# Norms applied behind the products, scan terms added in pairs and later state copies in a hybrid convolution, scan, attention and expert kernel

## The chip, the cores and the metric

The kernel runs on one core of a Trainium2 chip. The core has TensorE (PE, with its weight loads shown apart as PEld), VectorE (DVE), ScalarE (ACT), GpSimd (POOL) and SyncE (SP), which issues the transfers. All data is 32-bit floating point. The metric is the device time of one execution in microseconds (us); lower is better.

## The reference

The input is four images of 128 channels, 64 by 64 pixels. Two layers follow. In the first, per image:

```python
xn  = _ln(xp, ln_w, ln_b)                    # after a group norm of x
h   = depthwise 3x3 convolution, _ln, gelu, 1x1 convolution; y = y + h
m   = _mamba(chunks of _ln(y)) + skip_scale * chunks
out = _ln(inp + cat, ln_w, ln_b) @ proj_w.T + proj_b
x   = x + out
```

The scan inside `_mamba` runs over 4096 pixels with 16 states for each of 64 inner channels, in four chunks of the channels:

```python
h = dA_t * h + dBu_t
y = jnp.einsum('bdn,bn->bd', h, C_t)
```

In the second, on tokens `t` (pixels by 128 channels):

```python
t = t + attention(_ln_t(t))                  # 4 heads, 4096 keys, softmax
n = _ln_t(t)
p = top 2 of softmax(n @ router_w + router_b), shares that sum to 1
t = t + sum over the two experts of p * (n @ expert_w[e] + expert_b[e])
```

`_ln` takes off the mean over the channels and multiplies by rstd = 1/sqrt(variance + eps). In the norm ahead of `proj_w`, weight and bias follow it; the norm ahead of the router and the experts has none.

## The kernel before

An image is cut into 8 blocks of 512 pixels (`BLK`), a block into `NT` = 4 tiles of 128. Four images make 32 blocks.

The main loop of the kernel counts *slots*. In each slot every engine gets its instructions in program order; `Queue` and `queued` (lines 428 to 448) keep that order on each engine. All instructions issued this way bear the profile's line L445, so groups are told apart by the names of tiles.

**The scan** is cut into 512 *units* `(b, i, p, n)`: image, block, half of the channels and pair of states. A unit takes two slots. In its even slot `driven` (DVE) makes `h` as a product of fetched rows and `du`, and `scan` (DVE) runs over 1025 columns: two states laid end to end. In its odd slot `read` (DVE) multiplies `h` by other rows into `hc`, 128 by 2 by 512. The decays `da` are two ScalarE exponentials, issued a slot or two ahead by `prepared`; `carried` copies the second state's start into `h`, and `kept` copies both end states out, at the end of the unit's even slot. The terms `hc` of 8 units sum in one PSUM tile `y`: `turned_on` (line 792) transposes four tiles of each half of `hc` with accumulation. Half 0 is due one slot after `read`, half 1 two slots after. When a group of 8 units is done, ScalarE copies `y` to `yT`, and a slot later `turned_back` transposes it and calls `summed_up`, whose first step `scanned` (DVE) reads the result.

**Attention** runs beside it, one group per slot, 1024 in all: four score products `sc` (PE), two exponentials `pT` of 128 by 1024 (ACT), and in the next slot the value products `av` (PE, eight half products). There are two score buffers. Attention for an image begins when its first blocks are `closed`, so it trails the scan; from `END`, 1024 slots, attention runs alone.

**Two lanes, X and Y,** carry all other work as generators; each half of `advance` runs a lane to its next `yield`. Per block, Y runs `first_norm`, `conv` and `inputs`, which makes the scan's inputs, with a chain of five POOL operations ending in `du`. X runs `closed` (line 816), which makes the output projection, the residual and keys, queries and values, and `finished` (line 1059), which applies the attention's output projection, the router and the experts. A lane has one PSUM tile, `work(lane)`. In `closed` and `inputs` the set `held` keeps the two lanes from using X's tile at once.

`normalised` (line 504) is the norm in both lanes: `bn_stats` and `bn_aggr` (DVE) on four tiles, `rs` and `shift` (DVE), the power -1/2 and a product on POOL, then, two yields on, four ScalarE activations into `xt`. Its caller transposes `xt`. `closed` uses it twice, `finished` once. In `closed` the first result is transposed, scaled by `lnw` and `lnb` into `f` (ACT), multiplied by `projT`, and added to `xr`, which holds x and `projb`. In `finished` the transposed result `xf` goes to the router `rw` and, times each expert's share, to `ew`. The shares go through DRAM (`shares`) to be spread over the partitions. The output `res` begins as a ScalarE copy of a PSUM tile, in which the biases `eb8` times the shares and the transposed `acc`, as products with the identity, are summed.

One order in an even slot, as issued: `da` (ACT), `driven` (DVE), X's second half, scores (PE), exponentials (ACT), `scan` (DVE), Y's first half, `turned_back`, `turned_on` (PE), Y's second half, `kept` (ACT), values (PE), X's first half.

Of the kernel before, what the change touches and what calls it, by code (L numbers as in the profile page):

```python
# [36 lines left out]
def conv_mamba_attn_moe_kernel(ctx: ExitStack, tc: tile.TileContext, t: dict):  # L37
# [65 lines left out]
    with (  # L103
        tc.tile_pool(name="bound", bufs=1) as bd,
        tc.tile_pool(name="ps_w", bufs=2, space=PSUM) as ps_w,
    ):
        pw = ps_w.tile([P, P], F32, name="pw")
        nc.tensor.matmul(pw, lhsT=xdt, rhs=dtT, start=True, stop=True)
        nc.vector.tensor_copy(wdt, pw)
        pw = ps_w.tile([P, P], F32, name="pw")  # L110
        nc.tensor.matmul(pw[0:1, :], lhsT=bvc, rhs=wp, start=True, stop=True)
        crow1 = bd.tile([1, C], F32, name="crow1")
        nc.vector.tensor_add(crow1, pw[0:1, :], bp)
        pw = ps_w.tile([P, P], F32, name="pw")
        nc.tensor.matmul(pw, lhsT=ones, rhs=crow1, start=True, stop=True)
        nc.vector.tensor_copy(crow, pw)

        sq = bd.tile([P, 2 * NH + 1], F32, name="sq")
        nc.vector.memset(sq, 0.0)
        bsq = bd.tile([DH, 2 * NH], F32, name="bsq")
        for i, (w, bias) in enumerate(((wqn, bqn), (wkn, bkn))):
            for h in range(NH):
                r = slice(DH * h, DH * h + DH)
                pw = ps_w.tile([P, P], F32, name="pw")
                nc.tensor.matmul(pw[0:DH, 0:DH], lhsT=w[:, r], rhs=w[:, r], start=True, stop=True)
                g = bd.tile([DH, DH], F32, name="g", bufs=2)
# [40 lines left out]
        nc.vector.tensor_copy(general, ok)  # L170
    setup.close()


# [327 lines left out]
    def by_tile(src):  # L501
        return src.rearrange("p (j c) -> p j c", c=P)

    def normalised(lane, src):


        st = small.tile([P, NT, 6], F32, name=f"st{lane}")
        mv = small.tile([P, NT, 2], F32, name=f"mv{lane}")
# [3 lines left out]
            vector.bn_aggr(out=mv[:, j, :], in_=st[:, j, :])  # L512
        rs = small.tile([P, NT], F32, name=f"rs{lane}")
        vector.tensor_scalar_add(rs, mv[:, :, 1], EPS)
        shift = small.tile([P, NT], F32, name=f"shift{lane}")
        vector.tensor_scalar_mul(shift, mv[:, :, 0], -1.0)
        gpsimd.tensor_tensor(rs, rs, mhalf, ALU.pow)
# [283 lines left out]
    def summed_up(b, i, p, y):  # L801
        scanned(b, i, p, y)
        done.add(("scan", b, i, p))
        if p == 1:
            lanes["X"].appendleft((("closed", b, i), closed(b, i), []))

    def turned_back(b, i, p, yT):
        y = ps_y.tile([P, BLK], F32, name="y")
        for j in range(NT):
            tensor.transpose(y[:, j * P : (j + 1) * P], yT[:, j * P : (j + 1) * P], ident)  # L810
        summed_up(b, i, p, y)

    vst = side.tile([P, NH, NT, 2 * DH], F32, name="vst")
    gpsimd.memset(vst[:, :, :, DH:], 1.0)
# [1 line left out]
    def closed(b, i):  # L816
# [25 lines left out]
        vector.tensor_add(cm, ps, cm)  # L842
        gpsimd.tensor_add(by_tile(xr), by_tile(xr), projb[:, None, :].to_broadcast([P, NT, C]))
        yield
        while held:
            yield
            yield
        held.add("closed")
        ps = transposed("X", by_tile(cm))
        yield  # L850
        xt = yield from normalised("X", by_tile(ps))
        held.clear()
        ps = transposed("X", xt)
        yield
        f = tmp("X", "f")
        scalar.activation(f, ps, AF.Identity, bias=lnb, scale=lnw)
        yield
        ps = work("X", [P, NT, C])
        for j in range(NT):
            mm(ps[:, j, :], f[:, j * P : (j + 1) * P], projT)  # L860
        yield
        tt = side.tile([P, NT, C], F32, name="tt")
        vector.tensor_add(tt, ps, by_tile(xr))
        send(tsave[b][:, s], tt.rearrange("p j c -> p (j c)"), 2)
        xt = yield from normalised("X", tt)

# [192 lines left out]
    def finished(b, qb, lane):  # L1059
# [18 lines left out]
            mm(ps[:, j, :], aT[:, j * P : (j + 1) * P], wp)  # L1078
        yield
        vector.tensor_add(acc, ps, acc)  # L1080
        xt = yield from normalised(lane, acc)
        ps = transposed(lane, xt)
        yield
        xf = tmp(lane, "xf")
        scalar.copy(xf, ps)
# [8 lines left out]

        yield

        pr = routed("pr")
        vector.tensor_add(pr, ps, rb[:, None, :].to_broadcast(wide))
# [28 lines left out]
        vector.tensor_mul(pr, pr, top1.to_broadcast(wide))  # L1127
        yield

        ps = work(lane)  # L1130
        for j in range(NT):
            tensor.transpose(ps[0:NE, j * P : (j + 1) * P], pr[:, j, :], ident)
        yield
        prT = tmp(lane, "prT")[0:NE, :]
        scalar.copy(prT, ps[0:NE, :])
        shares = dram.tile([NE, BLK], F32, name=f"shares{lane}")
        send(shares, prT)
        yield

        def share(e):  # L1140
# [10 lines left out]


        ps = work(lane)
        mm(ps, eb8, prT, True, False)
        for j in range(NT):
            mm(ps[:, j * P : (j + 1) * P], acc[:, j, :], ident, False, j == NT - 1)
        yield
        res = tmp(lane, "res")
        scalar.copy(res, ps)
        yield  # L1160
        ahead = deque(share(e) for e in (0, 2))
        yield
# [23 lines left out]
    def advance(lane, second):  # L1186
# [3 lines left out]
        while True:  # L1190
            if lane not in running:

                tasks = lanes[lane] if lanes[lane] or slot < END else lanes["X"]
                if not tasks or not all(k in done for k in tasks[0][2]):
                    return False

# [89 lines left out]
    def ends(unit):  # L1286
        return unit[3] == NST - 2

    waiting = None

    while slot < END or due or closing or waiting or left or later or lanes["X"] or running:
        at, odd = divmod(slot, 2)
        flush()
        if slot == 0:
# [6 lines left out]
        if unit and not odd:  # L1301
            h = h_of.pop(at)
            driven(unit, h, rows.pop((at, 0)))
        advance("X", True)
        group = next(groups, None)
        if group:
# [144 lines left out]
```

## Time and profile before

| | us |
|---|---|
| median of 3 runs | 5390.83 |
| lowest and highest of them | 5374.57, 5391.15 |
| the profiled execution's own time | 5380.67 |
| its span, first to last instruction | 5378.9 |
| first scan starts at | 101.1 |
| first score product at | 382.9 |
| last scan ends at | 4790.1 |

The mean granted TensorE clock is 0.951. The page in slices of 134.5 us (busy tenths) shows how the span falls into a start, a long even middle and an end without scans:

```profile
PE   4556898999999999999999999999999999999997
PEld 2333444444444444444444444444444444444443
DVE  4888767777777778877778778777777877751332
ACT  3456777888777788788877788787777787766553
POOL 2333233333322224223322324333322232310100
```

A line of the page's groups reads: line, engine, operation, what it writes and reads, shapes, count, then busy us and mean ns of one, then the idle time of the engine just before these instructions and what ended it. A line of waits reads: who waited for whom, us in total, times, longest.

### The profile page before, as it was taken

To read this page: it belongs to the slowest core of one execution; us is meant where nothing else is said; L and a number is where in the kernel's file an instruction comes from. 1 tells how busy PE (TensorE), PEld (TensorE's weight loads), DVE (VectorE), ACT (ScalarE), POOL (GpSimd) and SP (SyncE) were. 2 spreads that over 40 slices of the span, in tenths; PEclk is the share of its full clock that TensorE was granted. 3 is DMA by queue.
4 is the path that set the end of the run, shared out by engine and by line. 5 is a ranking of instruction groups with operands and counts; after the bars stand their busy time and mean duration, and the time that the engine had idled before them with its cause. 6 is when DMAs were issued, how large, how long until landed. Compare 5 with 4: busy or idle time off the path is not lost. (4 is left out here: it accounts for less than half of the span.)

```text
span 5378.9 us, 64061 instructions
## 1 busy us (share of the span) xinstructions
PE 4850.0 (90%) x21066; PEld 2366.3 (44%) x21066; DVE 3757.2 (70%) x5123; ACT 3926.8 (73%) x6117; POOL 1525.0 (28%) x1091
## 2 busy tenths in 40 slices
PE   4556898999999999999999999999999999999997
PEld 2333444444444444444444444444444444444443
DVE  4888767777777778877778778777777877751332
ACT  3456777888777788788877788787777787766553
POOL 2333233333322224223322324333322232310100
PEclk7677899999999999999999999999999999999998
DMA  3556567667666667666766667666766676655532
GB/s 95 176 186 208 197 205 242 231 228 240 232 209 215 218 218 258 225 223 233 257 216 213 217 221 251 233 207 240 270 205 202 207 237 218 239 191 174 174 138 70
DMA packets 451702, 1131.71 MB, mean 210 GB/s; under 512 B 51985, under 2 KB 135330, under 8 KB 451362
## 3 DMA queue, kind: packets, MB, share of 16 engines
q1 hardware_dynamic: 450194, 1126.74, 62.4%
q8 instruction: 169, 2.77, 0.2%
q14 instruction: 171, 1.40, 0.1%
q10 hardware_dynamic: 1168, 0.80, 0.0%
HBM read 967.12 MB, written 143.39 MB: 206 GB/s over the span
## 5 line engine op out<-in xcount | busy, mean ns | idle before, releaser
L445 ACT ACTIVATE pT<-sc 128x1024 f32<-128x1024 f32 x2048 | 1985.7, 1024 | 637.2 <-PE sc L445 635.5
L445 PE MATMUL av<-pT,v 128*64 128x512 f32 x8192 | 2011.1, 612 | 16.7 <-ACT avs L445 16.4
L445 PE MATMUL sc<-qs,ks 128*128 128x512 f32 x4096 | 1316.7, 440 | 134.4 <-ACT pT L445 82.1
L445 DVE TENSOR_TENSOR_SCAN h<-da,state,h 128x1025 f32<-128x1025 f32 x512 | 1275.5, 2491 | 198.2 <-ACT h L445 168.9
L445 PEld LDWEIGHTS sc<-qs,ks 128*128 128x128 f32 x4096 | 705.6, 192 | 835.6 <-ACT pT L445 376.0
L445 PEld LDWEIGHTS av<-pT,v 128*64 128x64 f32 x8192 | 503.4, 138 | 824.7 <-issue 780.0
L445 ACT ACTIVATE da<-delta,amat 128x512 f32<-128x512 f32 x1024 | 747.9, 731 | 4.5 <-POOL delta L445 2.6
L445 DVE TENSOR_TENSOR h<-rows,du 128x1024 f32<-128x1024 f32 x512 | 707.8, 1382 | 53.0 <-POOL du L445 28.5
L445 DVE TENSOR_TENSOR hc<-rows,h 128x1024 f32<-128x1024 f32 x512 | 700.9, 1369 | 18.2 <-PE y L445 4.4
L445 PE MATMUL y<-ident,hc 128*128 128x128 f32 x4096 | 639.5, 285 | 64.3 <-DVE hc L445 56.9
L445 PEld LDWEIGHTS y<-ident,hc 128*128 128x128 f32 x4096 | 523.5, 147 | 269.2 <-issue 116.7
L445 POOL TENSOR_TENSOR rsX<-rsX,mhalf 128x4 f32<-128x4 f32 x92 | 232.7, 2530 | 843.1 <-DVE shiftX L445 843.1
L445 ACT ACT_TABLE_LOAD x319 | 409.3, 1283 | 18.1 <-PE ps_Y L445 13.5
L445 POOL TENSOR_TENSOR rsY<-rsY,mhalf 128x4 f32<-128x4 f32 x100 | 171.5, 1715 | 795.7 <-DVE shiftY L445 795.7
L445 ACT COPY state<-h 128x2 f32<-128x2 f32 x448 | 87.8, 196 | 416.3 <-DVE h L445 412.4
L445 POOL TENSOR_TENSOR avs<-avs,prev 128x512 f32<-128x512 f32 x96 | 153.0, 1594 | 660.2 <-ACT avs L445 612.6
L445 POOL TENSOR_TENSOR zs<-xin,zs 128x512 f32<-128x512 f32 x64 | 105.0, 1640 | 806.5 <-DVE xin L445 797.2
L445 POOL TENSOR_SCALAR du<-e 128x512 f32<-128x512 f32 x64 | 130.3, 2035 | 554.6 <-ACT e L445 554.6
L445 DVE TENSOR_TENSOR share<-share,xf 128x1024 f32<-128x1024 f32 x128 | 177.9, 1390 | 150.9 <-DMA share<-sharesX 124.9
L445 PE MATMUL ps_X<-share,w_ew 128*128 128x512 f32 x432 | 214.5, 619 | 1.7
L445 DVE TENSOR_TENSOR res<-res,ps_X 128x512 f32<-128x512 f32 x108 | 73.4, 679 | 178.9 <-PE ps_X L445 126.9
L445 ACT ACTIVATE xt<-ps_Y,shiftY,rsY 128x128 f32<-128x128 f32 x380 | 143.0, 466 | 67.9 <-POOL shiftY L445 60.7
(238 smaller groups left out, 4415.9 us busy)
## 6 DMA issues: line engine op xcount, KB each, us to landing
rows<-bcd SPq DMA_DIRECT2D x1024, 512.0 KB
ks<-kd SPq DMA_DIRECT2D x192, 512.0 KB
qs<-qd SPq DMA_DIRECT2D x161, 512.0 KB
share<-sharesX SPq DMA_DIRECT2D x108, 512.0 KB
v<-vd SPq DMA_DIRECT2D x192, 256.0 KB
ks<-kd SPq DMA_DIRECT2D x128, 256.0 KB
avd<-avs SPq DMA_DIRECT2D x96, 256.0 KB
prev<-avd SPq DMA_DIRECT2D x96, 256.0 KB
```

The costliest lines, as they stand in the source:

```text
L445: return lambda *args, **kw: queued(op(*args, **kw))
```

## The change

1. **Weights centred, rstd at eviction.** In the setup, a matrix `cen` (identity less 1/128) multiplies `rw`, `ew` and `projT` (the last scaled by `lnw`); `lnb` times `projT` is added to `projb`. A product of such a weight with data that still has its mean gives the product of the centred data. `moments` is split off `normalised`; `spread` computes rstd alone.
2. In `closed`, the first norm's `xt`, its transposition and `f` go; `projT` multiplies `cm`, and four DVE steps multiply by rstd and add `xr`. The wait for `held` goes.
3. In `finished`, `xt` goes; `acc` itself is transposed to `xf`. The router's result is multiplied by rstd (DVE). Shares are made twice, plain (for the biases) and times rstd (for the experts), in one tile `both`, and transposed together. The four products of `acc` with the identity go: `res` is the bias product plus `xf`, on DVE.
4. **Pairs.** From slot `ALONE` = 64 on, POOL adds the two halves of `hc` and one half is transposed, due two slots after `read`, three for the first unit of a group. Before slot 64, half 0 of a group's first unit becomes due two slots later.
5. `kept` runs at the end of the unit's odd slot. `summed_up` runs a slot after `turned_back`.
6. Lane Y does not take a `closed` task of X's once the scans are over.

```diff
+        def centred(w, src):
+            n = w.shape[1]
+            for k in range(0, n, P):
+                pw = ps_w.tile([P, P], F32, name="pw")
+                m = min(P, n - k)
+                nc.tensor.matmul(pw[:, 0:m], lhsT=cen, rhs=src[:, k : k + m], start=True, stop=True)
+                nc.vector.tensor_copy(w[:, k : k + m], pw[:, 0:m])
...
+    def spread(lane, src):
+
+        mv, rs = moments(lane, src)
+        gpsimd.tensor_tensor(rs, rs, mhalf, ALU.pow)
+        return rs
...
-        while held:
-            yield
-            yield
-        held.add("closed")
         ps = transposed("X", by_tile(cm))
         yield
-        xt = yield from normalised("X", by_tile(ps))
-        held.clear()
-        ps = transposed("X", xt)
-        yield
-        f = tmp("X", "f")
-        scalar.activation(f, ps, AF.Identity, bias=lnb, scale=lnw)
+        rs = spread("X", by_tile(ps))
         yield
         ps = work("X", [P, NT, C])
         for j in range(NT):
-            mm(ps[:, j, :], f[:, j * P : (j + 1) * P], projT)
+            mm(ps[:, j, :], cm[:, j * P : (j + 1) * P], projT)
         yield
         tt = side.tile([P, NT, C], F32, name="tt")
-        vector.tensor_add(tt, ps, by_tile(xr))
+        for j in range(NT):
+            vector.scalar_tensor_tensor(
+                tt[:, j, :], ps[:, j, :], rs[:, j : j + 1], xr[:, j * P : (j + 1) * P],
+                ALU.mult, ALU.add,
+            )
...
-        xt = yield from normalised(lane, acc)
-        ps = transposed(lane, xt)
+        rs = spread(lane, acc)
+        yield
+        ps = transposed(lane, acc)
...
-        mm(ps, eb8, prT, True, False)
-        for j in range(NT):
-            mm(ps[:, j * P : (j + 1) * P], acc[:, j, :], ident, False, j == NT - 1)
+        mm(ps, eb8, prT[0:NE, :])
         yield
         res = tmp(lane, "res")
-        scalar.copy(res, ps)
+        vector.tensor_add(res, ps, xf)
...
+        if summing:
+            summed_up(*summing)
+            summing = None
...
-            late = slot >= ALONE and unit[3] == 0
-            due.append((slot + 1 + late, unit, 0, hc[:, 0, :], False))
-            due.append((slot + 2, unit, 1, hc[:, 1, :], ends(unit)))
+            late = 2 * (unit[3] == 0)
+            if slot < ALONE:
+                due.append((slot + 1 + late, unit, 0, hc[:, 0, :], False))
+                due.append((slot + 2, unit, 1, hc[:, 1, :], ends(unit)))
+            else:
+                gpsimd.tensor_add(hc[:, 0, :], hc[:, 0, :], hc[:, 1, :])
+                due.append((slot + 2 + late // 2, unit, 0, hc[:, 0, :], ends(unit)))
         advance("Y", False)
         while closing and closing[0][0] <= slot:
-            turned_back(*closing.popleft()[1:])
+            summing = turned_back(*closing.popleft()[1:])
...
-        if unit and not odd:
+        if unit and odd:
             kept(unit, h)
```

More of the change, by code (lines that the diff above doesn't have):

```diff
@@ L170, in conv_mamba_attn_moe_kernel @@
         nc.vector.tensor_copy(general, ok)
+        cen = bd.tile([P, P], F32, name="cen")
+        nc.vector.tensor_scalar(cen, ident, 1.0 / C, None, ALU.subtract)
+        def centred(w, src):
[5 more added lines that the diff above has]
+                nc.vector.tensor_copy(w[:, k : k + m], pw[:, 0:m])
+        centred(rw, rw)
+        ewf = ew.rearrange("p e c -> p (e c)")
+        centred(ewf, ewf)
+        gain = bd.tile([P, C], F32, name="gain")
+        nc.vector.tensor_scalar_mul(gain, projT, lnw)
+        pw = ps_w.tile([P, P], F32, name="pw")
+        lnbs = bd.tile([P, P], F32, name="lnbs")
+        nc.vector.tensor_copy(lnbs, lnb.to_broadcast([P, P]))
+        nc.tensor.matmul(pw, lhsT=lnbs, rhs=projT, start=True, stop=True)
+        nc.vector.tensor_add(projb, pw, projb)
+        centred(projT, gain)
     setup.close()
@@ L502, in by_tile, with moments @@
         return src.rearrange("p (j c) -> p j c", c=P)
-    def normalised(lane, src):
+    def moments(lane, src):
         st = small.tile([P, NT, 6], F32, name=f"st{lane}")
@@ L514, in normalised @@
         vector.tensor_scalar_add(rs, mv[:, :, 1], EPS)
+        return mv, rs
+    def spread(lane, src):
+        mv, rs = moments(lane, src)
+        gpsimd.tensor_tensor(rs, rs, mhalf, ALU.pow)
+        return rs
+    def normalised(lane, src):
+        mv, rs = moments(lane, src)
         shift = small.tile([P, NT], F32, name=f"shift{lane}")
@@ L810, in turned_back @@
             tensor.transpose(y[:, j * P : (j + 1) * P], yT[:, j * P : (j + 1) * P], ident)
-        summed_up(b, i, p, y)
+        return b, i, p, y
     vst = side.tile([P, NH, NT, 2 * DH], F32, name="vst")
@@ L1095, in finished @@
         yield
+        both = routed("both", 2 * NE)
         pr = routed("pr")
-        vector.tensor_add(pr, ps, rb[:, None, :].to_broadcast(wide))
+        vector.tensor_mul(pr, ps, rs[:, :, None].to_broadcast(wide))
+        vector.tensor_add(pr, pr, rb[:, None, :].to_broadcast(wide))
         m = routed("m", 1)
@@ L1126, in finished @@
         vector.reciprocal(top1, top1)
-        vector.tensor_mul(pr, pr, top1.to_broadcast(wide))
+        vector.tensor_mul(both[:, :, 0:NE], pr, top1.to_broadcast(wide))
+        vector.tensor_mul(both[:, :, NE:], both[:, :, 0:NE], rs[:, :, None].to_broadcast(wide))
         yield
@@ L1131, in finished @@
         for j in range(NT):
-            tensor.transpose(ps[0:NE, j * P : (j + 1) * P], pr[:, j, :], ident)
+            tensor.transpose(ps[0 : 2 * NE, j * P : (j + 1) * P], both[:, j, :], ident)
         yield
-        prT = tmp(lane, "prT")[0:NE, :]
-        scalar.copy(prT, ps[0:NE, :])
+        prT = tmp(lane, "prT")[0 : 2 * NE, :]
+        scalar.copy(prT, ps[0 : 2 * NE, :])
         shares = dram.tile([NE, BLK], F32, name=f"shares{lane}")
-        send(shares, prT)
+        send(shares, prT[NE:, :])
         yield
@@ L1193, in advance @@
                 tasks = lanes[lane] if lanes[lane] or slot < END else lanes["X"]
+                if tasks and lane == "Y" and tasks[0][0][0] == "closed":
+                    return False
                 if not tasks or not all(k in done for k in tasks[0][2]):
@@ L1287, in ends @@
         return unit[3] == NST - 2
-    waiting = None
-    while slot < END or due or closing or waiting or left or later or lanes["X"] or running:
+    waiting, summing = None, None
+    while (
+        slot < END or due or closing or summing or waiting or left or later or lanes["X"] or running
+    ):
         at, odd = divmod(slot, 2)
```

## The prediction

> **What bounds the kernel now.** I read the busy shares of the page first, then a table of the span cut into stretches, then the waits of the long middle stretch, and last the timeline. The page, its busy shares and three of its costliest groups:
>
> ```profile
> PE 4850.0 (90%) x21066; PEld 2366.3 (44%) x21066; DVE 3757.2 (70%) x5123; ACT 3926.8 (73%) x6117; POOL 1525.0 (28%) x1091
> ...
> L445 PE MATMUL y<-ident,hc 128*128 128x128 f32 x4096 | 639.5, 285 | 64.3 <-DVE hc L445 56.9
> ...
> L445 ACT COPY state<-h 128x2 f32<-128x2 f32 x448 | 87.8, 196 | 416.3 <-DVE h L445 412.4
> L445 POOL TENSOR_TENSOR avs<-avs,prev 128x512 f32<-128x512 f32 x96 | 153.0, 1594 | 660.2 <-ACT avs L445 612.6
> ```
>
> See three things: TensorE is the fullest engine; ScalarE stands idle 412 us ahead of the state copies, waiting for the scan; a 128x512 addition on POOL takes 1.59 us. The stretches (length, then busy time of PE, PEld, DVE, ACT, POOL, then clock, DMA share, GB/s):
>
> ```profile
> 322.00:1000.00 678.00, 561.89 (x2380) 289.23 (x2379) 501.68 (x571) 484.87 (x806) 225.91 (x152) 0.90 0.65 215
> 1000.00:4790.00 3790.00, 3582.56 (x15970) 1748.73 (x15971) 2897.21 (x3811) 2995.06 (x4667) 1164.56 (x803) 0.98 0.67 227
> 4790.00:5303.00 513.00, 505.94 (x2069) 217.21 (x2066) 122.81 (x346) 300.50 (x364) 38.24 (x39) 1.00 0.43 144
> ```
>
> The middle stretch holds 398 of the 512 scan units (a unit is two slots), so a unit takes 3790/398 = 9.52 us, of which PE is busy 9.00, DVE 7.28, ACT 7.53. The last stretch is attention without scans, PE 99% busy. In the middle, who waits:
>
> ```profile
> ACT pT L445 <- PE sc L445: 400.6, 348, 9.3
> ...
> ACT state L445 <- DVE h L445: 257.9, 113, 5.1
> ...
> PE sc L445 <- ACT pT L445: 68.2, 152, 3.0
> ```
>
> ACT waits for PE six times longer than PE for ACT: PE sets the pace. Its work in one slot, from the timeline:
>
> ```profile
> 3001.60 1.48 PE L445 MATMUL sc<-qs,ks 128*128 128x512 f32 x4
> ...
> 3002.91 0.60 PE L445 MATMUL y<-ident,hc 128*128 128x128 f32 x4
> ...
> 3003.44 1.94 PE L445 MATMUL av<-pT,v 128*64 128x512 f32 x8
> ```
>
> From the start of the four y transpositions to the start of the next product pass 0.53 us. Start to start over the whole middle it is 450.6 us for 3188, so 0.141 us each. Busy times of PE overlap and are not summed here.
>
> And what two additions on POOL do to the taps beside them (two taps in each DVE line):
>
> ```profile
> 3302.31 1.51 DVE L445 SCALAR_TENSOR_TENSOR cm<-y,w_fc1w,cm 128x512 f32<-128x512 f32 x2
> ...
> 3303.84 2.24 POOL L445 TENSOR_TENSOR avs<-avs,prev 128x512 f32<-128x512 f32 x1
> ...
> 3304.88 3.45 DVE L445 SCALAR_TENSOR_TENSOR cm<-y,w_fc1w,cm 128x512 f32<-128x512 f32 x2
> ```
>
> Two taps take 1.51 us alone and 3.45 beside `avs` and the addition behind it: 0.97 more for each.
>
> **What the Trainium skill says.** "SBUF — State Buffer", Who interferes with whom: a VectorE instruction with two SBUF inputs contends with a GpSimd instruction that reads SBUF, and the later one blocks. The trace agrees in kind: of 512 `hc` products 288 had no POOL instruction beside them and took 1.22 us, with an earlier `zs` 2.30; the scan takes 2.35, after an earlier `tr` 3.31. The loss is 1.0 to 1.1 us, less than the 1.6 of the whole addition. "TensorE: Matmul & The Clock Gate", table at the top: ScalarE and VectorE queues are strict FIFO. The trace agrees: every ACT instruction after a state copy starts after it. "Perfetto Trace Analysis", Tensor Engine Instruction: TensorE's end times are estimated. That is why I use start to start. "GPSIMD Engine Reference", Engine selection: two-input elementwise work is about 2 times slower there; here 1.59 against DVE's 0.69, 2.3 times.
>
> **The change part by part.**
>
> *Pairs.* From slot 64 on, units 32 to 511, POOL adds the two halves of `hc` and PE transposes 4 tiles a unit, not 8. PE loses 4 x 0.141 = 0.563 us a unit: 398 x 0.563 = 224 in the middle, and 82 x 0.563 = 46 before it, of which I count half since PE is only 83% busy there. Together -247 us. POOL gains 480 x 1.6 = 770 us and goes to 42%. The sum is due two slots on, about 9 us; after `hc` (1.2 us) and the addition (1.6, to 2.2 when blocked) some 5 us are spare. At the end of `hc` POOL is busy in 39% of the units, 1.2 us on average, over 3.0 in 2%; the spare covers it. Without cover PE would wait in order.
>
> *The lock.* In 340 of the 480 units the next DVE instruction after `hc` is the product `h<-rows,du`; DVE idles 0.08 us in the mean behind `hc`. A window of 1.1 us behind `hc` is 88% filled by two-input instructions. So an addition costs DVE 0.88 x 1.08 = 0.95 us, 480 times 456 us.
>
> *Norm ahead of the projection.* Per block ACT loses four `xt` (0.46) and `f` (0.82); PE four transpositions, 0.53, over 32 blocks -17. The X lane has 91 norms, 59 of which no longer feed a waiting transposition; PE's waits for `xt` in X are 14 us in the middle, so -9. DVE: four 128x128 eviction steps from PSUM for one of 0.69. They are not in the trace; the nearest, bn_stats of that shape from PSUM, takes 0.28, a 128x512 step 0.75: between 4 x 0.28 and 4 x 0.75, I take 0.30 since the size is that of bn_stats. With the shift gone (0.16) +0.35.
>
> *Router and experts.* PE loses eight half products with `acc` at 0.114 (start to start): 0.91 x 32 = -29. Transposing 16 columns for 8 streams the same identity: nothing. ACT loses 4 x 0.48 + 0.59, DVE gets 0.19 + 0.19 + 0.68 - 0.16 = +0.90. Both parts: DVE +1.25 a block of 16 units, 0.08 a unit; ACT -5.2 a block, 166 us in all. `rstd` is used two slots after POOL's pow is issued; pow takes 1.7 to 2.5, hidden.
>
> No transfer is added; those of `closed` go to SP's queue two slots earlier and those of `finished` one, in the same number.
>
> *State copies late; sum read a slot later.* The copy stands an odd slot later, behind the exponentials; DVE has one more slot for the scan. ACT's 258 us of waiting in the middle go. PE feels it in `sc` behind `pT`, 68 us, and `av` behind `avs`, 15: at most 84, at least nothing; I take half, -42, since long ACT lane work delays `pT` too. DVE's wait for `y` ahead of `xin` (99 us in the middle) moves behind a finished transposition.
>
> *Small ends.* Setup: 11 products and some 14 DVE steps of 128x128, beside idle engines: 0 to 8 us, I take +4. First 322 us: ACT waits 58 us for scans, PE 31 for `hc`; -8. `closed` is two slots shorter, begins one later, and doesn't wait for `held`: attention starts a few slots earlier and an attention slot less remains at the end, -6. Last norms: -6.
>
> *What is late next.* PE needs 9.00 - 0.56 - 0.09 (46 us over 512 units) = 8.35 us a unit; DVE 7.28 + 0.08 + 0.95 = 8.31. Both queues are in order and meet in every slot through the lanes (product, eviction, product). PE now loses 0.52 a unit to waits with DVE 76% full; with DVE at 95% it will lose more. From nothing to 0.6 a unit; I take 0.30, 398 x 0.30 = +120 us, since `y` has slack and only lane steps wait.
>
> Sum: -247 - 26 - 29 - 42 + 120 - 16 = -240. Against the profiled execution's 5380.67 that is 5140. The median of the runs shown is 10 higher, which is inside their spread; I add nothing.
>
> **Rivals.**
> - *VectorE takes over.* For it: 8.31 us of work, and DVE's waits in the middle, 2.24 a unit, include ones that PE's pace doesn't make (shares from DMA 108 us). Against it: most end with PE. If 1.0 a unit stays in series, 9.3: the middle gains 0.22 x 398 = 88, the rest some 40: 5250.
> - *ScalarE's loop with the score buffers.* Two `sc` buffers tie `sc` of a slot to the exponentials of the last. For it: weight loads for `sc` wait for `pT` 258 us in the middle. Against it: ACT has 7.53 - 0.33 = 7.2 a unit. If the even slots give their 0.28 a unit back, +112, and the copies bring nothing, +42, with the stall at DVE half (-60): 5235.
> - *Slower: the shared port at full price.* In the blocked pair `hc` to `h<-rows,du`, the addition costs DVE its whole length, 1.65, as `avs` meets two operations in a row, and 0.8 of waits remain: 7.36 + 1.65 + 0.8 = 9.8 a unit, +0.29 x 398 = 115, less 55 for the rest: 5440. It decides from about 9.65 a unit, so from lock plus waits of 2.3.
>
> **How the numbers follow.** Forecast 0.60, VectorE takes over 0.18, ScalarE's loop 0.09, slower 0.11, nothing changes 0.02. The forecast's own range is 5000 (no stall at DVE, all of the 84) to 5230. To leave out no more than 2 in 10 I go to 5310: above it 0.13, below 0.05. A measurement here can tell some 0.3%, 16 us, from no change. Faster 0.85, within 0.04, slower 0.11.
>
> **What would show it.** Half the `y` transpositions (about 2176); `h<-rows,du` at a mean near 2.1 us for 1.38; DVE over 90% and PE still over 92% in the middle; ACT's wait ahead of `state` nearly gone; a unit of some 8.95 us. Wrong if PE waits long for `hc` behind POOL, or if the unit stays at 9.5 with DVE full.

## The result and the profile after

The changed kernel takes 5371.73 us in the median of 14 runs (5364.37 to 5378.38); the kernel before, run beside it 14 times, takes 5382.64. The ratio is 0.998, with an interval of 0.9972 to 0.9988. That is 0.2% faster: inside the 0.3% that the prediction set as the bound of no change, 232 us above its forecast of 5140, and outside its range of 5000 to 5310.

The busy shares of the page, and the groups that the change was to move (L467 is the line that was L445):

```profile
PE 4627.1 (86%) x18784; PEld 2096.2 (39%) x18784; DVE 4062.5 (76%) x5265; ACT 3800.0 (71%) x5797; POOL 2475.1 (46%) x1507
...
L467 DVE TENSOR_TENSOR_SCAN h<-da,state,h 128x1025 f32<-128x1025 f32 x512 | 1422.1, 2778 | 107.7 <-ACT h L467 74.9
L467 POOL TENSOR_TENSOR hc<-hc 128x512 f32<-128x512 f32 x480 | 925.8, 1929 | 1182.1 <-DVE hc L467 1117.5
...
L467 DVE TENSOR_TENSOR h<-rows,du 128x1024 f32<-128x1024 f32 x512 | 781.5, 1526 | 53.6 <-POOL du L467 28.2
...
L467 PE MATMUL y<-ident,hc 128*128 128x128 f32 x2176 | 359.3, 294 | 144.8 <-POOL hc L467 110.6
```

Two of these groups as they were before the change:

```profile
L445 DVE TENSOR_TENSOR_SCAN h<-da,state,h 128x1025 f32<-128x1025 f32 x512 | 1275.5, 2491 | 198.2 <-ACT h L445 168.9
L445 DVE TENSOR_TENSOR h<-rows,du 128x1024 f32<-128x1024 f32 x512 | 707.8, 1382 | 53.0 <-POOL du L445 28.5
```

The transpositions `y` fell from 4096 to 2176 as announced, and TensorE's share fell with them, to 86%. The work left TensorE, and its place was taken by idle time, not by the next work. VectorE has 305 us more to do, though few of its instructions are new: the scan takes 2778 ns in the mean (2491 before), the product `h<-rows,du` 1526 (1382). `y` now waits for POOL, which was not seen before.

The stretches, in the columns of the table shown in the prediction:

```profile
322.00:1000.00 678.00, 522.55 (x1992) 243.34 (x1992) 523.10 (x566) 463.99 (x764) 360.70 (x220) 0.86 0.63 211
1000.00:4790.00 3790.00, 3409.99 (x14191) 1536.08 (x14190) 3183.58 (x3965) 2913.66 (x4453) 1989.10 (x1165) 0.97 0.68 228
4790.00:5303.00 513.00, 496.58 (x1972) 205.17 (x1968) 116.60 (x320) 285.48 (x319) 31.20 (x27) 0.99 0.43 143
```

In the middle PE is 90% busy (95% before) and DVE 84% (76%), so no single engine is full. Who waits there:

```profile
ACT pT L467 <- PE sc L467: 552.2, 416, 9.0
...
PE y L467 <- POOL hc L467: 91.9, 38, 7.0
...
PE ps_X L467 <- DVE share L467: 57.2, 65, 4.4
PE sc L467 <- DMA ks<-kd: 50.0, 19, 9.3
...
ACT state L467 <- DVE h L467: 34.9, 11, 11.2
...
DVE tt L467 <- POOL rsX L467: 25.6, 5, 6.2
```

The wait that the late state copy was to remove is nearly gone (258 us before, 35 now). In its place stand several waits of 25 to 92 us on PE and DVE, for each other and for POOL. The timeline shows where DVE's extra time comes from:

```profile
3001.28 1.22 DVE L467 TENSOR_TENSOR h<-rows,du 128x1024 f32<-128x1024 f32 x1
...
3001.50 2.12 POOL L467 TENSOR_TENSOR hc<-hc 128x512 f32<-128x512 f32 x1 [3.48 <-DVE hc L467]
...
3002.60 3.18 DVE L467 TENSOR_TENSOR_SCAN h<-da,state,h 128x1025 f32<-128x1025 f32 x1
...
3010.88 2.35 DVE L467 TENSOR_TENSOR_SCAN h<-da,state,h 128x1025 f32<-128x1025 f32 x1
```

POOL's addition began beside the product, which had begun first, and took 2.12 us (the shortest are near 1.3). It was still running when the scan began: 3.18 us, against 2.35 for the scan that meets none.

A table for what follows, worked out from the traces: means over the units from 129 to 449, in us per unit. "Occupied" is the time from the start of one TensorE instruction to the next, without the idle time between; "DVE busy" is the time in which at least one of its instructions runs, as in the stretches; "groups" counts the attention groups that begin in these 320 units, "left" those that begin after the last scan has begun.

| kernel | unit | TensorE occupied | TensorE idle | DVE busy | granted clock | groups | left |
|---|---|---|---|---|---|---|---|
| before | 9.59 | 9.05 | 0.54 | 7.34 | 0.979 | 637 | 136 |
| after | 9.46 | 8.48 | 0.98 | 8.01 | 0.966 | 624 | 147 |
| e4, no pairs | 9.29 | 8.77 | 0.51 | 7.37 | 0.980 | 625 | 147 |
| e2, half the terms left out | 9.04 | 8.37 | 0.67 | 7.35 | 0.975 | 624 | 147 |
| e8, norms alone | 9.76 | 9.02 | 0.74 | 7.40 | 0.961 | 636 | 134 |
| e6, late copies alone | 9.32 | 8.81 | 0.51 | 7.16 | 0.982 | 623 | 151 |
| e14, no pairs, order and phase mended | 9.23 | 8.87 | 0.36 | 7.39 | 0.986 | 637 | 137 |

A unit became 0.13 us shorter, but that is hardly a gain. The same 320 units hold 12 attention groups fewer than before. A group takes about 3.0 us of TensorE's time (6.06 us of `sc` and `av` for the two groups of a unit, by starts), so 12 of them make an estimated 0.12 us a unit: work put off to the end. The last scan ends 36 us earlier (4753.9 for 4790.1), the stretch behind it is 20 us longer (608.3 for 588.8), and the difference is the 17 us by which the profiled span fell. Units can be compared between kernels only where the groups agree.

### The profile page after: what moved, and what is told of

The parts are those of the page before. It is cut to its first block, busy times and chain, and to the rows that moved or that the text cites. A ratio compares the mean times of both kernels' runs of the same rounds, so it can differ in the third digit from the quotient of the medians.

```text
span 5362.2 us, 60222 instructions
## 1 busy us (share of the span) xinstructions
PE 4627.1 (86%) x18784; PEld 2096.2 (39%) x18784; DVE 4062.5 (76%) x5265; ACT 3800.0 (71%) x5797; POOL 2475.1 (46%) x1507
## 4 chain that ended last, share of the span: by engine, by line
PE 37%; DVE 26%; ACT 9%; issue 9%; POOL 9%; DMA 8%; SPq 1%; DVEq 0%; POOLq 0%; ACTq 0%
PE av L467 16%; DVE h L467 12%; PE sc L467 9%; PE ps_X L467 5%; PE ps_Y L467 5%; DVE hc L467 3%; ACT pT L467 3%; POOL du L467 3%; ACT L467 2%; DVE cm L467 2%; PE y L467 2%; DMA ks<-kd 2%; DMA rows<-bcd 2%; POOL hc L467 1%; POOL ln L467 1%
## 5 line engine op out<-in xcount | busy, mean ns | idle before, releaser
L467 ACT ACTIVATE pT<-sc 128x1024 f32<-128x1024 f32 x2048 | 1984.7, 1023 | 809.9 <-PE sc L467 807.7
L467 PE MATMUL av<-pT,v 128*64 128x512 f32 x8192 | 2036.7, 619 | 2.9 <-ACT avs L467 2.9
L467 DVE TENSOR_TENSOR_SCAN h<-da,state,h 128x1025 f32<-128x1025 f32 x512 | 1422.1, 2778 | 107.7 <-ACT h L467 74.9
L467 POOL TENSOR_TENSOR hc<-hc 128x512 f32<-128x512 f32 x480 | 925.8, 1929 | 1182.1 <-DVE hc L467 1117.5
L467 PE MATMUL sc<-qs,ks 128*128 128x512 f32 x4096 | 1311.4, 439 | 146.4 <-ACT pT L467 75.2
L467 PEld LDWEIGHTS sc<-qs,ks 128*128 128x128 f32 x4096 | 708.7, 192 | 894.1 <-ACT pT L467 400.6
L467 PEld LDWEIGHTS av<-pT,v 128*64 128x64 f32 x8192 | 506.4, 138 | 912.5 <-issue 871.3
L467 DVE TENSOR_TENSOR h<-rows,du 128x1024 f32<-128x1024 f32 x512 | 781.5, 1526 | 53.6 <-POOL du L467 28.2
L467 ACT ACTIVATE da<-delta,amat 128x512 f32<-128x512 f32 x1024 | 742.8, 730 | 7.0 <-POOL delta L467 4.0
L467 DVE TENSOR_TENSOR hc<-rows,h 128x1024 f32<-128x1024 f32 x512 | 706.6, 1380 | 45.4 <-DVE h L467 19.1
L467 PE MATMUL y<-ident,hc 128*128 128x128 f32 x2176 | 359.3, 294 | 144.8 <-POOL hc L467 110.6
L467 POOL TENSOR_TENSOR rsY<-rsY,mhalf 128x4 f32<-128x4 f32 x100 | 141.2, 1412 | 594.9 <-DVE shiftY L467 325.2
L467 PEld LDWEIGHTS y<-ident,hc 128*128 128x128 f32 x2176 | 290.5, 152 | 271.3 <-POOL hc L467 130.2
L467 POOL TENSOR_TENSOR rsX<-rsX,mhalf 128x4 f32<-128x4 f32 x92 | 184.7, 2007 | 327.4 <-DVE rsX L467 258.9
L467 POOL TENSOR_TENSOR avs<-avs,prev 128x512 f32<-128x512 f32 x96 | 177.2, 1845 | 278.2 <-ACT avs L467 273.8
L467 PE MATMUL ps_X<-share,w_ew 128*128 128x512 f32 x432 | 217.1, 626 | 57.2 <-DVE share L467 57.2
L467 ACT ACTIVATE xt<-ps_Y,shiftY,rsY 128x128 f32<-128x128 f32 x380 | 143.4, 463 | 172.5 <-POOL shiftY L467 165.3
L467 POOL TENSOR_TENSOR zs<-xin,zs 128x512 f32<-128x512 f32 x64 | 119.9, 1874 | 240.8 <-DVE xin L467 240.8
L467 POOL TENSOR_SCALAR du<-e 128x512 f32<-128x512 f32 x64 | 176.0, 2750 | 107.5 <-ACT e L467 107.5
L467 ACT COPY avs<-av 128x512 f32<-128x512 f32 x160 | 94.5, 591 | 138.3 <-PE av L467 96.0
L467 DVE SCALAR_TENSOR_TENSOR cm<-y,w_fc1w,cm 128x512 f32<-128x512 f32 x192 | 189.9, 989 | 3.4
```

Source lines behind the costliest of these rows:

```text
L467: return lambda *args, **kw: queued(op(*args, **kw))
```

## The experiments

The theories at the start: the additions cost more than the halved transpositions are worth (through the shared port, through POOL's time, or because `y` waits for the sum); or the pairs pay, and the norms and the new order of tasks lose it. "The kernel before" was run beside each; all ratios are to it, with a 95% interval.

### What the pairs are worth

e4 is the changed kernel without pairs; e2 is the changed kernel without the addition, so the terms of the second half of `hc` are left out of `y` from slot 64 on: halved transpositions for nothing.

```diff
# e4
-            late = 2 * (unit[3] == 0)
-            if slot < ALONE:
-                due.append((slot + 1 + late, unit, 0, hc[:, 0, :], False))
-                due.append((slot + 2, unit, 1, hc[:, 1, :], ends(unit)))
-            else:
-                gpsimd.tensor_add(hc[:, 0, :], hc[:, 0, :], hc[:, 1, :])
-                due.append((slot + 2 + late // 2, unit, 0, hc[:, 0, :], ends(unit)))
+            late = slot >= ALONE and unit[3] == 0
+            due.append((slot + 1 + late, unit, 0, hc[:, 0, :], False))
+            due.append((slot + 2, unit, 1, hc[:, 1, :], ends(unit)))
# e2, against the changed kernel
-                gpsimd.tensor_add(hc[:, 0, :], hc[:, 0, :], hc[:, 1, :])
```

> The kernel after with the pairs undone: all 4096 transpositions, due times of before, no additions on POOL; norms and late copies stay. If the pairs gain nothing or lose: 5300 to 5370, so at or below the kernel after. If they gain the 247 us of TensorE's work and something else eats it (order, norms): 5450 or more.

> The kernel after without the 480 additions on POOL, so that the second state of each pair is left out of the sum from slot 64 on: TensorE's saving without its price. Theory 'TensorE sets the pace and the additions eat the gain' (by queue or lock): 5150 to 5220, TensorE's idle time in the middle back from 380 to some 230 us, VectorE's busy time back to about 3800. Theory 'ScalarE loop' (TensorE's freed time comes back as waits for the exponentials, whatever POOL does): 5330 to 5370.

e4 took 5293.95 us (0.9838 [0.9822, 0.9855]), e2 5182.16 (0.9629 [0.9613, 0.9645]). Without pairs the change would have been 1.6% faster; the pairs take 78 us back. And even at no cost at all they bring 112, not 247. Between e4 and e2 TensorE's time in `y` falls by 0.54 us a unit, close to the predicted 0.563. But 0.14 of it comes back in its other products (by their starts, 0.05 of it in `sc`, 0.03 in `av`, 0.02 in `xt`), and 0.16 as idle time, so that the unit is 0.25 us shorter. The waits of e2 in 1000 to 4700 us show what was next in line:

```profile
PE ps_X L467 <- DVE bothX L467: 63.2, 22, 7.6
PE sc L467 <- ACT pT L467: 61.5, 147, 2.2
PE sc L467 <- DMA ks<-kd: 51.6, 17, 9.3
```

In e4 these three are 48.7, 35.0 and 39.0. TensorE comes earlier to products whose inputs other engines and transfers deliver.

### Which part of the addition costs

Three kernels split the addition's cost. In e13 POOL writes zeros three times into the half of `hc` that nobody reads (about the same POOL time, and the second terms are left out as in e2). In e12 the addition runs as in the changed kernel, but its sum goes into the unread half, so `y` doesn't wait for it and has half the terms. e10 puts the fills into the half that is read, so `y` waits for POOL and scan terms are replaced by zeros.

```diff
-                gpsimd.tensor_add(hc[:, 0, :], hc[:, 0, :], hc[:, 1, :])
# e13
+                for _ in range(3):
+                    gpsimd.memset(hc[:, 1, :], 0.0)
# e12
+                gpsimd.tensor_add(hc[:, 1, :], hc[:, 0, :], hc[:, 1, :])
# e10
+                for _ in range(3):
+                    gpsimd.memset(hc[:, 0, :], 0.0)
```

> As the fills with zeros, but into the second half of hc, which nobody reads, with the first half transposed as it is (second terms left out): POOL is as busy, reads nothing, and TensorE doesn't wait for it. If POOL's occupancy alone delays the lanes (norms behind the fills): 5235 to 5262. If the 80 us were TensorE's wait for POOL: 5182 to 5205.

> The kernel after with POOL's sum written into the second half of hc, which nobody reads, while TensorE transposes the first half as it is: the scan's second term of each pair is left out from slot 64 on. The additions load POOL and hold the port as before, but no transposition waits for POOL. If TensorE's wait for the sum costs what lies between half the terms (5182) and the fills (5262): 5285 to 5305. If the wait merely moves elsewhere, as it did with the later due time: 5340 to 5375.

> The kernel after with each addition replaced by three fills of the same 128x512 half with zeros on POOL (0.53 us each in the profile before, 1.6 us together): the same queue, the same waits of the transpositions, but POOL reads nothing; the scan's terms from slot 64 on are left out. Theory 'lock': the scan and the products of VectorE are back at their times without additions, VectorE's busy time at 3760 to 3800, 5190 to 5250. Theory 'POOL queue': 5330 to 5375, with TensorE waiting for hc as in the kernel after.

e13 took 5250.21 us (0.9755 [0.9739, 0.9771]), e12 5368.43 (0.9974 [0.9964, 0.9983]), e10 5261.77 (0.9776 [0.9759, 0.9792]). Set in a row, each step adds one thing:

| step | what is added | us |
|---|---|---|
| e4 to e2 | half of `y` goes | -112 |
| e2 to e13 | POOL's time | +68 |
| e13 to e12 | POOL reads SBUF beside DVE | +118 |
| e12 to the changed kernel | `y` waits for the sum | +3 |
| together | | +78 |

The last step is too small to be told from nothing: the intervals of e12 and the changed kernel overlap. (With fills, from e13 to e10, the same wait costs 12.) The groups by shape of e10 show that the fills leave the scan alone:

```profile
L467 POOL MEMSET hc<- 128x512 f32 x1440 | 762.5, 530 | 1269.8 <-DVE hc L467 1189.4 <-PE ps_X L467 14.0 <-PE y L467 8.4
...
L467 DVE TENSOR_TENSOR_SCAN h<-da,state,h 128x1025 f32<-128x1025 f32 x512 | 1251.2, 2444 | 131.4 <-ACT h L467 100.1
```

Three fills of 0.53 us keep POOL busy for 1.59 us a unit, and the scan, at 2444 ns, is no longer than in e2, where POOL does neither (2489). The additions are longer than the fills (1.93 us), so some of the 118 is POOL's time: at e13's rate, 68 us for 761 us of fills, 163 us more would cost an estimated 15. The Trainium skill, "SBUF — State Buffer", Who interferes with whom, says that a DVE instruction with two inputs in SBUF contends with a GpSimd instruction that reads SBUF, and not with one that only writes it. Both halves of it are seen here: the scan takes 2778 ns in the mean with the additions, 2444 with the fills.

Two attempts to evade the cost: e9 makes every sum due a slot later than the changed kernel's usual one, e3 puts the addition on VectorE.

```diff
# e9
-                due.append((slot + 2 + late // 2, unit, 0, hc[:, 0, :], ends(unit)))
+                due.append((slot + 3, unit, 0, hc[:, 0, :], ends(unit)))
# e3
-                gpsimd.tensor_add(hc[:, 0, :], hc[:, 0, :], hc[:, 1, :])
+                vector.tensor_add(hc[:, 0, :], hc[:, 0, :], hc[:, 1, :])
```

> The kernel after with every pair's transpositions due three slots after the product instead of two, some 4.5 us more for POOL; additions and port stay as they are. Theory 'POOL queue': TensorE's waits for hc (92 us in the middle, 2.9 us once a block behind the chain that makes du) go, 5270 to 5300. Theory 'lock' (VectorE stretched by the additions holds the rest back): the waits move to other products of the lanes, 5345 to 5375.

> The kernel after with the 480 additions on VectorE (about 0.69 us each, 331 us of busy time) in place of POOL: no queue on POOL, no lock from them. Theory 'POOL queue': TensorE's 92 us of waiting for hc are gone, 5240 to 5300, though VectorE is as full as with the lock. Theory 'lock, VectorE full': 331 us of work for some 230 us of blocking, 5360 to 5450.

e9 took 5364.06 us (0.9959 [0.9945, 0.9973]). The 92 us of `y` waiting for `hc` are gone, yet only 8 us are won: 66 us of waits for `hc`'s buffer now stand ahead of DVE's `hc`, and some of PE's waits ahead of lane work grow (for `xt` in lane Y from 25 to 66 us). A wait with little behind it moves on when it is removed, as e12's 3 us say too. e3 took 5343.89 (0.9931 [0.9915, 0.9948]): 28 less than on POOL, though VectorE is then busy for 8.17 us a unit. Here an addition paid openly on VectorE is cheaper than one on POOL that makes others wait; both are worse than none (e4).

e5 makes the pairs alone, on the kernel before:

> The kernel before with the pairs alone (additions on POOL, new due times, no norms, no late copies). In the kernel with norms and late copies the pairs cost 78 us. If lock and occupancy of POOL outweigh TensorE's saving whatever else is done: 5440 to 5500. If ScalarE's waits for the scan, which the additions lengthen, add to it: over 5500. If TensorE's saving counts for more where TensorE is fullest: 5330 to 5380.

It took 5401.78 us (1.0043 [1.0027, 1.006]): 20 us slower. Pairs lose with the old norms too.

### The norms and the late copies, each alone

e8 has the norm parts on the kernel before: the changed kernel with the `due` lines of e4, `kept` in the even slot, and `summed_up` called at once (Y's guard stays). e6 is the kernel before with the two moves only, the state copies and `summed_up` (and Y's guard of part 6).

```diff
# e8, against e4
-            summing = turned_back(*closing.popleft()[1:])
+            summed_up(*turned_back(*closing.popleft()[1:]))
...
-        if unit and odd:
+        if unit and not odd:
# e6, against the kernel before
+        if summing:
+            summed_up(*summing)
+            summing = None
...
-            turned_back(*closing.popleft()[1:])
+            summing = turned_back(*closing.popleft()[1:])
...
-        if unit and not odd:
+        if unit and odd:
```

> The kernel before with the norm parts of the change alone (centred weights, rstd at eviction, res on VectorE): no pairs, state copies and sums where they were, so the closing task goes first again. If the norms make all of the 88 us that the kernel without pairs gained: 5285 to 5310. If the late copies carry half of it (42 us in the prediction): 5325 to 5345. If in the old order of tasks rstd waits on POOL behind the chain for du: 5350 or more.

> The kernel before with the later state copies and the later sum alone. The prediction's term: 42 us less, 5335 to 5345, ScalarE's wait ahead of the copies from 412 to under 60 us. If ScalarE's waiting never reached TensorE: 5375 to 5390. With the swapped tasks of lane X costing ten slots: 5385 to 5410.

e8 took 5457.99 us (1.0136 [1.0114, 1.0158]), e6 5329.74 (0.9898 [0.988, 0.9917]). So the norms, which take products from TensorE and ScalarE, make the kernel before 75 us slower, and the two moves make it 53 faster. POOL's timeline in e8 shows why the norms lose:

```profile
2586.20 2.05 POOL L467 TENSOR_SCALAR du<-e 128x512 f32<-128x512 f32 x1
2588.33 1.29 POOL L467 TENSOR_TENSOR du<-e,du 128x512 f32<-128x512 f32 x1
2589.70 3.34 POOL L467 TENSOR_TENSOR ln<-ln,du 128x512 f32<-128x512 f32 x1
2593.12 2.13 POOL L467 TENSOR_TENSOR delta<-delta,ln 128x512 f32<-128x512 f32 x1
2595.33 1.32 POOL L467 TENSOR_TENSOR du<-delta,xin 128x512 f32<-128x512 f32 x1
2596.61 2.00 POOL L467 TENSOR_TENSOR rsX<-rsX,mhalf 128x4 f32<-128x4 f32 x1
2598.70 1.49 POOL L467 TENSOR_TENSOR shiftX<-shiftX,rsX 128x4 f32<-128x4 f32 x1
```

And the other engines in the same stretch of e8:

```profile
2589.56 0.16 DVE L467 TENSOR_SCALAR shiftX<-mvX 128x4 f32<-128x4 f32 x1
...
2600.22 1.65 ACT L467 ACTIVATE xt<-tt,shiftX,rsX 128x128 f32<-128x128 f32 x4 [7.31 <-POOL shiftX L467]
...
2600.76 1.64 PE L467 MATMUL ps_X<-ident,xt 128*128 128x128 f32 x4 [6.43 <-ACT xt L467]
```

VectorE has the statistics of `closed`'s second norm ready at 2589.7. The power needs POOL, whose queue is in the middle of lane Y's chain of five operations to `du`; it starts 7 us later. ScalarE's `xt` stands in its queue 7.31 us, and TensorE, in order too, 6.43. Because `closed` is now two slots shorter, its second norm meets this chain in every block. The waits in 1000 to 4700 us count it:

```profile
ACT xt L467 <- POOL shiftX L467: 166.8, 24, 9.3
PE ps_X L467 <- ACT xt L467: 146.8, 24, 8.0
```

Before the change, in the middle (1000 to 4790 us):

```profile
ACT xt L445 <- POOL shiftX L445: 29.4, 37, 4.0
PE ps_X L445 <- ACT xt L445: 14.0, 15, 3.0
```

### The order of lane X and the phase against POOL

An output task (`finished`) may start in lane X only in slots 2 to 17 of a block's 32. Before, `closed` was handed over in slot 2 as well and went first, from slot 2 to 13. In the changed kernel `summed_up` comes a slot later, so the output task is first and, once there are such tasks, `closed` runs in nearly every block from slot 17 to 26. By image 1 keys come too late for the attention. The stretches of the changed kernel, of score products `sc` and what feeds on them alone (busy of PE, PEld, ACT, then clock, DMA share, GB/s):

```profile
2090.00:2138.00 48.00, 11.93 (x36) 6.38 (x36) 17.81 (x19) 0.93 0.80 274
2142.00:2190.00 48.00, 1.20 (x3) 1.04 (x4) 1.92 (x2) 0.63 0.68 236
```

In the second stretch hardly any attention ran: its slots went by without a group. They are made up at the end, among the 147 groups left instead of 136. e1 moves the gate by the same slot; e11 does that in e4.

```diff
-                    and not 2 <= slot % (2 * NST) < NST + 2
+                    and not 3 <= slot % (2 * NST) < NST + 3
```

> One number changed in the kernel after: an output task may start in lane X from slot 3 of each 32, not from slot 2, so that the closing task, which the change hands over one slot later, goes first again. Theory 'order' (the swapped tasks cost the attention 10 to 11 slots, that then run alone at the end at 3.0 us each): 1184 slots again for 1194, 30 to 60 us less, 5310 to 5340. Theory 'POOL queue' (most of the loss is TensorE behind the additions on POOL) and theory 'lock': within 35 us of the kernel after, since the additions stay.

> Norms and late copies without pairs, and the closing task first again in lane X (start of output tasks from slot 3 of 32). Theory 'phase' (the closing task is two slots shorter, and its second norm now asks for POOL while the chain for du holds it, once a block): slower than without this edit though ten slots are won, 5320 to 5380, with waits for rsX or shiftX of 5 us or more about 25 times. Theory 'order' alone: 5260 to 5275.

e1 took 5365.55 us (0.997 [0.9959, 0.998]), e11 5275.21 (0.9801 [0.9785, 0.9818]). Groups left fall to 135 in both, and the stretch behind the last scan gets 32 and 38 us shorter. But the scans, with these groups among them again, end 28 and 19 us later, so that only 6 and 19 us arrive. In e1 the power again falls behind the `du` chain, in every block: DVE's `tt` waits 151.7 us for POOL's `rsX`, ACT's `xt` 156.3 for `shiftX`, 25 times each. To test that, e14 delays the short `closed` by the slots that it had lost (e11 with four more yields, two slots), and e15 does the same with pairs (e1 with them):

```diff
         gpsimd.tensor_add(by_tile(xr), by_tile(xr), projb[:, None, :].to_broadcast([P, NT, C]))
         yield
+        for _ in range(4):
+            yield
         ps = transposed("X", by_tile(cm))
```

> As the run without pairs and the closing task first, with four more yields (two slots) in the closing task ahead of its first transpositions, so that its second norm comes where it came in the kernel before. Theory 'phase': the waits for POOL go, and 5255 to 5285, the fastest of all so far. If the norms are slow in the old order for another reason: as without the yields.

> The kernel after with the closing task first again and two slots later ahead of its transpositions, as in the fastest run so far (5232), but with the pairs. If the pairs' loss is theirs (lock and occupancy): 5300 to 5335, 70 to 100 above. If it came from the order of the tasks: 5150 to 5230.

e14 took 5232.01 us (0.9719 [0.9702, 0.9735]): two slots of doing nothing make e11 43 us faster. Waits for the norm's POOL results in 1000 to 4700 us, first e11:

```profile
ACT xt L467 <- POOL shiftX L467: 79.3, 25, 5.0
DVE tt L467 <- POOL rsX L467: 48.6, 19, 4.4
```

In e14 the second line is gone and the first is this:

```profile
ACT xt L467 <- POOL shiftX L467: 25.8, 24, 3.6
```

e15 took 5295.59 (0.9844 [0.9828, 0.9861]): 70 less than e1. With the order and the phase mended the pairs still cost 5295.59 - 5232.01 = 64 us. e14, the change without pairs, is the fastest full version here, 2.8% below the kernel before.

Last, e16 is e6 with the moved gate, to see whether its gain is the copies' or the swapped order's.

> The kernel before with late copies and the late sum, and the closing task first again. If the swapped tasks cost the late copies their ten slots: 5285 to 5310, 20 to 45 less than without this edit (5330). If the swapped order was an advantage in other places: 5325 to 5350.

It took 5376.05 us (0.9987 [0.9979, 0.9996]), 46 more than e6. So on the kernel before, the late copies and the late sum in the old order of tasks bring 6 us; the other 47 come with the swap, which lengthens the end by 15 groups and shortens the unit from 9.55 to 9.32, 0.13 of it by the estimate above because 14 groups are put off. With the new norms the same move of the gate helps (e4 to e11, -19). That fits a phase against POOL's chain which differs in the two: from 1000 to 4700 us ACT's `xt` waits 103 us for `shiftX` in e16, but 26 in e6 and in the kernel before. No run isolates it, so what the late copies are worth without this wait stays open.

## Why the prediction was wrong

One way from the kernel before to the changed one, by medians: late copies with their swap -53 (e6), norms on top of them -36 (to e4), pairs on top of both +78. Together -11. The parts aren't additive: alone, the norms cost 75.

The prediction's -240 and the measured -11 differ in three places. The halved transpositions brought 112 of 247 us, the additions cost 190 where a stall of 120 was put in, and everything else brought 89 of 113. That the last came so near is luck: in the old order of tasks its two parts, each alone, are +75 and -6.

- **Pairs, -247: the step that failed most.** The instructions were counted rightly: 2176, and 0.54 us a unit of TensorE's time (the 0.563 counts in 20 us of idle time over the middle). What failed is the assumption that TensorE's time is the unit's time, up to the one stall put in for VectorE. Even without any addition the halving was worth 112: of the 0.54 us, 0.16 came back as TensorE's idle time and 0.14 in its other products.
- **The lock, 0.95 us a unit: too dear as busy time, and put at the wrong instruction.** Product and scan together grew by (1526 - 1382 + 2778 - 2491)/1000 x 512 = 221 us; with 192 taps at 989 ns for 804, 256 us, not 456. The scan took most of it, the product was expected to. By the rule that the prediction quotes the later one blocks, and in 242 of 302 meetings of product and addition the product had begun first; it took 1.41 us in these, and 2.18 in the other 60, against 1.22 with nothing on POOL beside it. In 193 of 228 meetings of scan and addition the addition was first, and the scan took 3.16 us, about 0.8 more than a free one. A single collision is nearly as dear as predicted; there were fewer of them.
- **The stall, +120: too small, and laid to one cause of two.** It was the only charge for the additions in the sum, as waits with a full VectorE. The runs show 118 where POOL reads beside VectorE and 68 more for POOL's time alone, +186 without the 3 for the wait of `y`. "The spare covers it" missed 92 us of waits, but e12 shows that little hangs on them. Left out was who else queues on POOL: the powers of the lanes' norms stand behind the additions in order. From e2 to e13, in 1000 to 4700 us, ACT's waits for `shiftX` and `shiftY` rise from 44 to 74 us, DVE's `tt` for `rsX` from 12 to 26, and PE's waits by 40 in all. That this makes up the whole of the 68 isn't shown.
- **Norms, -26 and -29: right in what they remove, wrong in what they move.** "`closed` is two slots shorter" was booked as a gain in attention slots. It shifted the second norm onto the `du` chain (e8), and e14 shows that two idle slots repair it there (they were not tried in e8 itself). "pow hidden" failed for the same reason: the power's own time was hidden, but not the queue ahead of it (in e1 `tt` waits 6 us for `rsX` in every block). The four eviction steps took 1.12 us together, close to the four times 0.30 that were taken.
- **Late copies, -42: the wait went as said** (412 us ahead of `state` to 96, over the whole run), but in the old order the change was worth 6 (e16), with the waits for `shiftX` risen beside it.
- **"Begins one later", -6: the sign was wrong.** The prediction followed the length of `closed`, not the gate that decides between it and the output task. The swap left 11 more groups, and the stretch behind the last scan got 20 us longer, not shorter.

Of the signs that the prediction named, the halved `y` and the vanished wait ahead of `state` came. The product's mean is 1.53 us for the 2.1 that were to show the lock, PE is 90% busy in the middle for over 92, DVE 84% for over 90, and a unit takes 9.46 us for 8.95.

Of the rivals, the slower one (5440) is nearest in number and named the shared port, but the lock cost 256/480 = 0.53 us an addition and not its 1.65. "VectorE takes over" expected 8.31 us of work and 1.0 of waits in series; the runs show 8.01 of work and 1.45 of the rest in a unit of 9.46. Both missed the POOL queue. "Nothing changes" is what happened to the total, but as gains and losses that cancel.

## What to carry to other kernels

Before work is moved from the fullest engine, run the kernel once with the term left out and nothing in its place: that shows the gain at no cost, and here it was under half of the engine time saved. (Half of `y` was left out in the changed kernel's order alone; what that is worth in e14's order was not run.) When a task gets shorter or starts a slot later, ask which long chain holds the in-order queue at its new time, and which gate was set for the old one; mending both was worth 62 us here (e4 to e14). An elementwise step on POOL is not free because POOL is idle: here 480 of them cost 118 us by reading beside VectorE, and 68 by taking POOL's time.

## What was not expected of the hardware

How long one instruction is held up can be read off. Of the scans in the changed kernel, 95 met a single POOL instruction, an addition already running and with over 0.1 us to go. Each took longer than the free scan's 2.35 us by what was left of the addition, less 0.19 to 0.20 us. So the scan waits for the rest of the addition, not for all of it; in the timeline above, 1.02 us were left and 0.83 were lost.

TensorE's granted clock has only two values in the 320 units of the table, full and half, and half comes in stretches of 3.41 us or a multiple of it. They add up to 126 us in the kernel before, 208 in the changed one, 242 in e8 and 82 in e14. In e8 TensorE stalls for over 6 us in 18 of these 20 blocks, and each time 6.8 or 10.2 us at half clock begin within the stall; in the changed kernel the longest stretch, 37.6 us, lies where the attention slots went by empty. The sum of idle time alone doesn't set the mean: e8 idles 0.74 us a unit at 0.961, the changed kernel 0.98 at 0.966. How long a gap must be for it was not worked out.

POOL's power on 128 by 4 numbers took about 1.0 us where no VectorE instruction ran beside it, and 2.0 to 3.1 beside a scan.
